# When a last convolution's two products run: the order of work in the inverse stage of a four-layer image kernel

## The chip, the core and the metric

One Trainium2 chip, one of its cores. The metric is the device time of one execution in microseconds (us); lower is better. The time before is a median of three runs, and the profile is of one further execution.

## The reference, cut to what matters

```python
def conv(x, z, ..., bias, L):              # layers 0, 1 and 3
    hx = _implicit_filter(z, Xw1, ..., deltas)
    hy = _implicit_filter(z, Yw1, ..., deltas)
    k = einsum('ijk,imk->ijmk', hx, hy)    # a separable filter for each channel
    ...
    y = irfft2(rfft2(x) * rfft2(k) / fft_size)[..., :L, :L]
    return y + x * bias[:, None, None]

def mix(x, v, conv_w, tau):                # layer 2
    f1 = haar2d(x)
    acc = 0
    for i in range(2):
        f4 = einsum('bchw,oc->bohw', f1 * v[i], conv_w[i])
        acc = acc + sign(f4) * relu(abs(f4) - tau[i])
    return haar2d(acc, inverse=True) + x

x = conv(x); x = conv(x); x = mix(x); x = conv(x)
```

x is (4, 64, 256, 256) in float32: 4 batches of 64 channels, each an image of 256 x 256. A convolution with a separable causal filter is two triangular Toeplitz products, one along each axis, with the channel's own filters.

## The kernel before, in words

**Tiling and stages.** A channel's image is a tile of 128 partitions x 2 x 256. A last convolution (layer 3, `last`, line 598) of one channel has five steps. The first product (`first`, line 256, due under the name "a3") contracts the image `u` with one of the channel's two Toeplitz filters into a PSUM bank `pa`; ScalarE copies it to SBUF as `a` ("a3 copy", line 267). The second product (`second`, line 271, "y3") contracts `a` with the other filter into a bank `py`; VectorE adds the image times its bias ("y3 sum", line 284), and ScalarE's queue starts the output's transfer ("out", line 602). Each product is `contract` (line 250): two halves, each with a matmul of 256 columns (line 253) and one of 128 (line 254). In the trace each of these is two passes, so a product is eight matmul records.

The work goes by batch. `convolutions` does layers 0 and 1 of a batch and the forward Haar transform, and leaves coefficients in DRAM (`coef`) and the images in `keep`. `mixing` mixes channels. `inverse` transforms back and does the last convolution. While batch b is mixed, layers 0 and 1 of batch b+1 run between its steps; the last eight channels of that are stretched over the first 36 ticks or so of the inverse stage of b. These late channels bring the steps "split" (ScalarE rounds to `sp`, line 361), "rest" (VectorE, line 366), "down" (a matmul into `pz`, line 373) and "away" (ScalarE copies `pz` to `co`, line 385, and SyncE's queue stores it), all due at n.73 of every third tick.

**The inverse stage** (`inverse`, line 509) has a tick for each of the 64 channels c, beginning at `start`. Steps of one channel, with the tick that they are due at: "sooner" c - 0.8 (SyncE's queue loads the filter tile `t`, line 244); "early" c - 0.4 (it loads `r`, line 515); "fetch" c + 0.414 (ScalarE gathers the channel's coefficients from `z` to `zc`, line 525); "rows" c + 1.071 (TensorE, lines 532 and 533, into `pw`); "join" c + 1.433 (VectorE, lines 554 to 558, makes the image `u`); then the last convolution. The first 16 channels have two steps more ("halves", "cols", lines 536 to 549), and their join and all after it are a tick later. Between these, VectorE does levels of the Haar transform on `z` (lines 291 and 292) for later channels.

In batches 0, 1 and 2 the channels 2, 5, 8, ... (`put_off`) do no last convolution here: `aside` puts `u` in DRAM (line 562), and `convolution` (line 605) does these 63 during the mixing of batch 3. So in three ticks there are two last convolutions. In batch 3 nothing is put off and each tick has one.

**What sets the order.** The author gives each step a due time in ticks, from the table `PLACE` and, for the last convolution, a shift by the channel's place in its group of three. All steps are sorted by due time and issued in that order (line 659). The framework turns this into one order per engine; there an instruction that isn't ready may be passed by a later one that is, so the due times act as priorities. After that each engine runs its own order and waits at each instruction. DMA triggers stand in the order of the engine that issues them: outputs and `late` in ScalarE's, loads and stores of `keep` and `coef` in SyncE's.

**Buffers that matter.** Four PSUM banks (tag "mm") serve all products, `pz` and "cols"; two pairs of banks serve rows and mixing. The copies `a` have two buffers ("mid"), images `u` five ("y"), filter tiles six ("toep"), and `r` three. The output tile of "y3 sum" and the coefficient tile of "away" share two buffers (tag "co").

Of the kernel before, what the change touches and what calls it, by code (L numbers as in the profile page):

```python
# [98 lines left out]
def conv_seq_kernel(ctx, tc, x, fz, fw, bias, decay, haar, haar_row, factors, vt, taut, wmix, out):  # L99
# [141 lines left out]
    def toeplitz(layer, c, name):  # L241

        t = tp.tile([P, 2, S], F32, name=name, tag="toep")
        nc.sync.dma_start(t, ap(pads[layer], c * 2 * ROW, [[1, P], [ROW, 2], [1, S]]))
        return t
# [48 lines left out]
    def level(n, chunk, begin=0, count=None):  # L294

        count = n if count is None else count
        v = z.rearrange("p n s x c -> p n s (x c)")[:, chunk].rearrange("p (j e s) x -> p j e s x", e=2, s=P // 2 // n)
        halve(v[:, begin : begin + count, 0, 0, :], v[:, begin : begin + count, 1, 0, :])

    def butterfly():  # L300

        v = z.rearrange("p n s (h k) c -> p n s h k c", k=2)
        for h in range(2):
            halve(v[:, :, 0, h, 0, :], v[:, :, 0, h, 1, :])
# [6 lines left out]
    def at(time, run, unit):  # L311
        events.append((time, len(events), run, unit))
# [196 lines left out]
    def inverse(b, start, put_off):  # L509

        st = {}

        def early(c):
            r = mx.tile([P, 2, 2, P], F32, name=f"r_{b}_{c}", tag="f", bufs=3)
            nc.sync.dma_start(r, keep[b][c])
            st[c]["r"] = r

        def sooner(c):
            st[c] = {}
            if c not in put_off:  # L520
                st[c][2] = toeplitz(2, c, f"t2_{b}_{c}")

        def fetch(c):
            a = mx.tile([P, 2, 2, P], F32, name=f"zc_{b}_{c}", tag="mag")
            nc.scalar.copy(a.rearrange("p h k i -> p (h k) i"), z[:, c // 16, :, :, c % 16].rearrange("p i x -> p x i"))  # L525
            st[c]["z"] = a

        def rows(c):
            a = st[c]["z"]
            ps = psx.tile([P, 2, 2, 2, P], F32, name=f"pw_{b}_{c}", tag="mix")[:, 0]  # L530
            for m in range(2):
                nc.tensor.matmul(ps[:, 0, m, :], a[:, 0, m, :], hsinv, start=True, stop=True)  # L532
                nc.tensor.transpose(ps[:, 1, m, :], a[:, 1, m, :], ident)  # L533
            st[c]["pw"] = ps

        def halves(c):
            w = st[c]["w"] = mx.tile([P, 2, 2, 2, P], F32R, name=f"w_{b}_{c}", tag="f4")
            ps = st[c]["pw"]
            nc.scalar.copy(w[:, 0], ps)
            nc.vector.tensor_tensor(w[:, 1], ps, w[:, 0].bitcast(F32), ALU.subtract)  # L540

        def cols(c):
            ps = psm.tile([P, 2, 2, P], F32, name=f"pu_{b}_{c}", tag="mm")
            flat = "p e m w -> p (e m w)"
            for i in range(2):
                nc.tensor.matmul(
                    ps.rearrange(flat), hb, st[c]["w"][:, i].rearrange(flat), start=(i == 0), stop=(i == 1)
                )
            st[c]["pw"] = ps

        def join(c):
            ps = st[c]["pw"]
            t = io.tile([P, 2, 2, P], F32, name=f"t_{b}_{c}", tag="res", bufs=BUFS["res"])
            nc.vector.scalar_tensor_tensor(t, st[c]["r"], 0.5, ps, ALU.mult, ALU.add)  # L554
            u = io.tile([P, 2, S], F32, name=f"u_{b}_{c}", tag="y", bufs=BUFS["y"])
            v = u.rearrange("p m (w e) -> p m w e", e=2)
            nc.vector.tensor_add(v[:, :, :, 0], t[:, 0], t[:, 1])  # L557
            nc.vector.tensor_sub(v[:, :, :, 1], t[:, 0], t[:, 1])  # L558
            st[c]["u"] = u

        def aside(c):
            nc.scalar.dma_start(late[b, c], st.pop(c)["u"])

        along = start - groups - 3

        def when(tick, n, chunk, *span):
            at(tick + PLACE["level"], lambda _: level(n, chunk, *span), 0)

        at(along + 11 + PLACE["level"], lambda _: butterfly(), 0)
        for chunk in range(1, 4):  # L570
            turn = start + 16 * (chunk - 1)
            for n in (1, 2, 4, 8):
                when(along + 12 + 3 * chunk if b + 1 < B else turn, n, chunk)
            when(turn + 1, 16, chunk)
            for i in range(2):
                when(turn + 2 + 2 * i, 32, chunk, 16 * i, 16)
            for i in range(4):
                when(turn + 6 + 2 * i, 64, chunk, 16 * i, 16)

        for c in range(C):  # L580
            for name, stage in zip(("sooner", "early", "fetch", "rows"), (sooner, early, fetch, rows)):
                at(start + c + PLACE[name], stage, c)
            turn = start + c
            if c < 16:
                at(start + c + PLACE["halves"], halves, c)
                at(start + c + PLACE["cols"], cols, c)
                turn += 1
            at(turn + PLACE["join"], join, c)
            if c in put_off:
                at(turn + PLACE["aside"], aside, c)  # L590
            else:
                shift = (0.0, -0.32) if c % 3 == 0 else (0.5, 0.18)
                if not put_off:
                    shift = (0.0, -0.5)
                for name, stage in zip(("a3", "a3 copy", "y3", "y3 sum", "out"), last(b, st)):
                    at(turn + PLACE[name] + shift[name[0] != "a"], stage, c)

    def last(b, st):
        return [
            *first(b, st, "u", 2, "a3"),  # L600
            *second(b, st, "a3", 2, "u", "y3", "co"),
            lambda c: nc.scalar.dma_start(out[b, c].rearrange("(k p) w -> p k w", p=P), st.pop(c)["y3"]),  # L602
        ]
# [19 lines left out]
    put_off = range(2, C, 3)  # L623
# [22 lines left out]
    for b in range(B):  # L646
        mixing(b, start, N_ACT[b])
        end = start + groups + 3
        if b + 1 < B:
            ready = convolutions(b + 1, spread(ahead, end + 2), in_parts=range(C), border=end)  # L650
        else:
            convolution(
                [(i, c) for i in range(B - 1) for c in sorted(put_off)], spread(start - 2, end + 2, (B - 1) * len(put_off))
            )
        inverse(b, end, put_off if b + 1 < B else ())

        start = max(end + C, ready + 3)
        ahead = start - 3
# [114 lines left out]
```

## Time and profile before

| | |
|---|---|
| median of 3 runs | 2916.31 us (2914.98 to 2917.72) |
| the profiled execution | 2915.48 us, its span 2913.7 us |
| granted TensorE clock | 1.0 |
| busy over the span: TensorE, VectorE, ScalarE, GpSimd | 2837.4, 2504.6, 2081.6, 329.1 us |
| inverse stage, first `zc` to last `zc`: batch 0 | 865.6 to 1056.6 us |
| batch 1 | 1517.7 to 1710.7 us |
| batch 2 | 2171.9 to 2365.9 us |
| batch 3 | 2662.4 to 2879.3 us |
| a copy `a` (line 267), fetch `zc` (line 525) | 0.587, 1.101 us (medians) |

How to read it: a row of the profile's groups has the line, the engine, the operation, what it writes and reads, and how often; then its busy time and the mean of one; then the idle time of that engine just before these instructions, and what ended most of it. PE is TensorE's matmuls, PEld its loading of weights, DVE is VectorE, ACT is ScalarE. Matmul records overlap by some 0.16 us[...].

### The profile page before, as it was taken

To read this page: it belongs to the slowest core of one execution; us is meant where nothing else is said; L and a number is where in the kernel's file an instruction comes from. 1 tells how busy PE (TensorE), PEld (TensorE's weight loads), DVE (VectorE), ACT (ScalarE), POOL (GpSimd) and SP (SyncE) were. 2 spreads that over 40 slices of the span, in tenths; PEclk is the share of its full clock that TensorE was granted. 3 is DMA by queue.
4 is the path that set the end of the run, shared out by engine and by line. 5 is a ranking of instruction groups with operands and counts; after the bars stand their busy time and mean duration, and the time that the engine had idled before them with its cause. 6 is when DMAs were issued, how large, how long until landed. Compare 5 with 4: busy or idle time off the path is not lost. (4 is left out here: it accounts for less than half of the span.)

```text
span 2913.7 us, 52472 instructions
## 1 busy us (share of the span) xinstructions
PE 2837.4 (97%) x16566; PEld 2548.3 (87%) x16566; DVE 2504.6 (86%) x4263; ACT 2081.6 (71%) x4950; POOL 329.1 (11%) x644
## 2 busy tenths in 40 slices
PE   8999999999999999999999999999999999999998
PEld 6899998888888898988898898988898898888887
DVE  4655558999999779999998779999998789999974
ACT  2333348999995558999986558999986568887443
POOL 0111111121120001212111001212111000000000
PEclk9999999999999999999999999999999999999999
DMA  5877777666677886776778886777778898876675
GB/s 163 259 231 229 231 236 218 205 207 205 200 209 231 277 251 199 212 214 209 211 215 252 265 249 200 213 213 207 212 215 255 260 266 230 238 228 204 206 227 168
DMA packets 599367, 649.77 MB, mean 223 GB/s; under 512 B 48465, under 2 KB 517044, under 8 KB 598964
## 3 DMA queue, kind: packets, MB, share of 16 engines
q1 hardware_dynamic: 519860, 562.09, 66.4%
q10 hardware_dynamic: 79232, 84.34, 8.2%
q8 instruction: 134, 2.20, 0.3%
q14 instruction: 141, 1.16, 0.1%
HBM read 426.77 MB, written 219.48 MB: 222 GB/s over the span
## 5 line engine op out<-in xcount | busy, mean ns | idle before, releaser
L253 PE MATMUL py<-t,a 128*128 128x256 f32 x3072 | 929.8, 384 | 32.1 <-ACT a L267 28.8
L267 ACT COPY a<-pa 128x512 f32<-128x512 f32 x768 | 491.4, 640 | 569.2 <-PE pa L254 511.3
L465 ACT ACTIVATE f<-px,vt 128x64 f32<-128x64 f32 x2816 | 622.2, 408 | 93.2 <-DVE f L460 93.0
L254 PEld LDWEIGHTS py<-t,a 128*128 128x128 f32 x3072 | 583.4, 190 | 79.4
L254 PE MATMUL py<-t,a 128*128 128x128 f32 x3072 | 590.1, 274 | 0.0
L253 PEld LDWEIGHTS py<-t,a 128*128 128x128 f32 x3072 | 494.9, 191 | 91.2 <-ACT a L267 59.7
L441 PE MATMUL px<-wb,f 128*128 128x256 f32 x2048 | 490.4, 381 | 11.4 <-ACT f L465 11.2
L441 PEld LDWEIGHTS px<-wb,f 128*128 128x128 f32 x2048 | 367.7, 190 | 56.7 <-ACT f L465 17.9
L343 POOL TENSOR_TENSOR sd<-less 128x128 f32<-128x128 f32 (+4 forms) x320 | 186.4, 583 | 1874.5 <-DVE less L342 1492.8
L469 ACT ACTIVATE mag<-f 128x1024 f32<-128x1024 f32 x256 | 304.3, 1189 | 20.8 <-DVE z L486 20.2
L476 DVE TENSOR_TENSOR mag<-mag,vt 128x1024 f32<-128x1024 f32 x256 | 311.7, 1218 | 5.0 <-ACT mag L469 4.0
L525 ACT COPY zc<-z 128x512 f32<-128x512 f32 x256 | 279.7, 1101 | 49.5 <-PE pw L533 38.0
L253 PE MATMUL pa<-t,y 128*128 128x256 f32 x1024 | 308.2, 383 | 5.6 <-DVE y L284 4.7
L480 DVE SCALAR_TENSOR_TENSOR mag<-mag,f 128x1024 f32<-128x1024 f32 x256 | 312.2, 1220 | 0.5 <-ACT f L472 0.4
L253 PE MATMUL pa<-t,x 128*128 128x256 f32 x1024 | 305.8, 380 | 0.0
L366 DVE TENSOR_TENSOR sp<-sd,sp 128x512 fp32r<-128x512 f32 x256 | 178.8, 698 | 146.7 <-ACT sp L361 144.2
L472 ACT ACTIVATE f<-f 128x1024 f32<-128x1024 f32 x256 | 291.5, 1139 | 3.2
L253 PE MATMUL pa<-t,u 128*128 128x256 f32 x772 | 231.4, 381 | 1.5 <-PE pw L533 0.7
L284 DVE SCALAR_TENSOR_TENSOR y<-x,bsb,py 128x512 f32<-128x512 f32 x256 | 189.5, 740 | 41.6 <-PE py L254 40.6
L284 DVE SCALAR_TENSOR_TENSOR y<-u,bsb,py 128x512 f32<-128x512 f32 x193 | 143.7, 745 | 91.2 <-PE py L254 70.1
L254 PEld LDWEIGHTS pa<-t,x 128*128 128x128 f32 x1024 | 194.6, 190 | 26.3
L254 PEld LDWEIGHTS pa<-t,y 128*128 128x128 f32 x1024 | 194.5, 190 | 26.3
(72 smaller groups left out, 4440.6 us busy)
## 6 DMA issues: line engine op xcount, KB each, us to landing
t<-pad SPq DMA_DIRECT2D x768, 256.0 KB, 4.1
x<-in_x SPq DMA_DIRECT2D x256, 256.0 KB, 3.8
coef<-co SPq DMA_DIRECT2D x256, 256.0 KB, 3.2
f<-coef SPq DMA_DIRECT2D x256, 256.0 KB, 3.2
r<-keep SPq DMA_DIRECT2D x256, 256.0 KB, 3.9
out_y<-y ACTq DMA_DIRECT2D x256, 256.0 KB, 4.1
keep<-sums SPq DMA_DIRECT2D x256, 128.0 KB, 2.8
keep<-sd SPq DMA_DIRECT2D x256, 128.0 KB, 2.9
```

The lines of the kernel that those rows point to most:

```text
L253: nc.tensor.matmul(ps[:, m, :], src[:, 0, m * P : (m + 1) * P], t[:, ::-1], start=True, stop=False)
L254: nc.tensor.matmul(ps[:, m, P:], src[:, 1, m * P : (m + 1) * P], t[:, : P - 1 : -1], start=False, stop=True)
L267: nc.scalar.copy(a, s["p" + new])
L284: nc.vector.scalar_tensor_tensor(y, s[res], bsb[:, layer, c : c + 1], s["p" + new], ALU.mult, ALU.add)
L343: engine.tensor_tensor(t[:, :, :, half:length], v[..., 0], v[..., 1], ALU.subtract)
L441: nc.tensor.matmul(ps[:, q, h, :], f[:, q, h * P : (h + 1) * P], wb.rearrange("p r n -> p (r n)"), start=True, stop=True,)
L465: nc.scalar.mul(f4[:, j], px[:, j], scale(g, 0)[:, j : j + 1])
L469: nc.scalar.activation(mag, st[g]["f4"], AF.Abs)
L472: nc.scalar.activation(st[g]["f4"], st[g]["f4"], AF.Sign)
L476: nc.vector.tensor_sub(mag, mag, over(g, 1, 16))
L480: nc.vector.scalar_tensor_tensor(mag, mag, 0.0, st[g]["f4"], ALU.max, ALU.mult)
L525: nc.scalar.copy(a.rearrange("p h k i -> p (h k) i"), z[:, c // 16, :, :, c % 16].rearrange("p i x -> p x i"))
```

## The change

Only the shifts of the last convolution's due times are changed.

```diff
-                shift = (0.0, -0.32) if c % 3 == 0 else (0.5, 0.18)
-                if not put_off:
-                    shift = (0.0, -0.5)
+                shift = (0.0, 0.0)
+                if put_off:
+                    shift = ((-0.27, -0.342), (0.23, 0.158))[c % 3]
                 for name, stage in zip(("a3", "a3 copy", "y3", "y3 sum", "out"), last(b, st)):
                     at(turn + PLACE[name] + shift[name[0] != "a"], stage, c)
```

The first number of a pair is for the first product and its copy, the second for the second product, its sum and the output. The due times that follow, for a channel c whose turn is c:

| | first product | its copy | second product and sum | output |
|---|---|---|---|---|
| batches 0 to 2, c % 3 = 0, before | c + 2.470 | c + 2.471 | c + 3.222 | c + 4.217 |
| after | c + 2.200 | c + 2.201 | c + 3.200 | c + 4.195 |
| batches 0 to 2, c % 3 = 1, before | c + 2.970 | c + 2.971 | c + 3.722 | c + 4.717 |
| after | c + 2.700 | c + 2.701 | c + 3.700 | c + 4.695 |
| batch 3, every c, before | c + 2.470 | c + 2.471 | c + 3.042 | c + 4.037 |
| after | c + 2.470 | c + 2.471 | c + 3.542 | c + 4.537 |

In batch 3 the second product of c is now due behind the first product of c + 1 (at c + 3.470), before it stood ahead of that. In batches 0 to 2, the copy of a first product with c % 3 = 0 is now due ahead of the fetch at c + 2.414, which it followed before, and the first product with c % 3 = 1 ahead of "split", "down" and "away" at c + 2.73, which it followed.

## The prediction, made before the changed kernel ran

> **What bounds the kernel now.** I read the page first, then the busy times by stage, then the waits of the last inverse stage, then the timeline of single ticks. The page names the engine:
>
> ```profile
> PE 2837.4 (97%) x16566; PEld 2548.3 (87%) x16566; DVE 2504.6 (86%) x4263; ACT 2081.6 (71%) x4950; POOL 329.1 (11%) x644
> ...
> L253 PE MATMUL py<-t,a 128*128 128x256 f32 x3072 | 929.8, 384 | 32.1 <-ACT a L267 28.8
> ...
> L253 PEld LDWEIGHTS py<-t,a 128*128 128x128 f32 x3072 | 494.9, 191 | 91.2 <-ACT a L267 59.7
> ```
>
> TensorE has next to no slack, and what idle time it has stands before `py`, the second product, waiting for ScalarE's copy `a` of the first. To see how much idle there is and where, I took the starts of all matmuls from the timeline and subtracted the spacing that unstalled ones show (0.216 us for 256 columns, 0.110 for 128). An unstalled product is 4 x 0.216 + 4 x 0.110 = 1.30 us, an unstalled `pw` (rows) 0.67. What is left over is TensorE's idle time: 123 us in the whole span, so no change of order can give more. The inverse stages, for which the change is made, hold: batches 0, 1, 2 from their 16th channel on (932 to 1062, 1582 to 1716, 2236 to 2371 us) 6.2, 9.6 and 10.7 us, of which the last third of each has 0.3, 0.3 and 0.9; their first 16 channels 6.2, 2.0 and 2.0; batch 3 (2662 to 2914) 3.8 for the first 16 channels and 22.2 for the rest. Batch 3 by stretches:
>
> ```profile
> 2713.00:2757.00 44.00, 40.96 (x253) 36.48 (x253) 42.25 (x69) 18.14 (x23) 0.00 (x0) 1.00 0.71 209
> 2757.00:2800.00 43.00, 42.09 (x269) 37.30 (x268) 41.23 (x68) 21.49 (x26) 0.00 (x0) 1.00 0.72 218
> 2800.00:2845.00 45.00, 44.24 (x283) 39.40 (x282) 27.97 (x52) 22.10 (x27) 0.00 (x0) 1.00 0.79 231
> 2845.00:2880.00 35.00, 34.35 (x215) 30.02 (x214) 21.67 (x40) 16.27 (x20) 0.00 (x0) 1.00 0.78 220
> 2880.00:2914.00 34.00, 25.24 (x146) 21.73 (x144) 11.84 (x20) 5.04 (x9) 0.00 (x0) 0.99 0.34 105
> ```
>
> The columns are the window, its length, then busy time of PE, PEld, DVE, ACT, POOL, the clock, DMA share, GB/s. To 2800 us VectorE is busy 83.5 of 87 us (the Haar levels on `z` run there): VectorE bounds. From 2800 it drops to 62% and TensorE bounds. My idle sums are 5.3, 3.6, 3.3, 3.3, 6.7. The waits of that part:
>
> ```profile
> DVE y L284 <- PE py L254: 47.1, 33, 2.9
> PEld py L253 <- ACT a L267: 18.2, 43, 0.9
> PE py L253 <- ACT a L267: 6.9, 12, 0.7
> ```
>
> and one tick with rows, then one after the last rows:
>
> ```profile
> 2881.75 0.38 PE L254 MATMUL pa<-t,u 128*128 128x128 f32 x2
> ...
> 2882.23 0.59 ACT L267 COPY a<-pa 128x512 f32<-128x512 f32 x1 [1.88 <-PE pa L254]
> ...
> 2882.87 0.70 PE L253 MATMUL py<-t,a 128*128 128x256 f32 x2
> ```
>
> ```profile
> 2893.71 0.30 PEld L253 LDWEIGHTS py<-t,a 128*128 128x128 f32 x2 [0.92 <-ACT a L267]
> 2893.71 0.70 PE L253 MATMUL py<-t,a 128*128 128x256 f32 x2 [0.73 <-ACT a L267]
> ```
>
> The reader is to see the order first product, rows, second product *of the same channel*. The copy starts 0.1 us after the product ends and takes 0.59; rows cover 0.67 of it, and 0.33 stay bare (0.23 of gap, and 0.10 for the first matmul after it). So the tick is 1.30 + 0.67 + 0.33 + 1.30 = 3.61 us, as the starts of `py` say (2839.49 to 2886.48 in 13 ticks). After the last rows nothing covers the copy, and the tick is 3.61 again with 1.0 us idle. In batches 0 to 2 there is a second pattern:
>
> ```profile
> 2288.98 0.75 DVE L284 SCALAR_TENSOR_TENSOR y<-u,bsb,py 128x512 f32<-128x512 f32 x1 [1.44 <-DMA coef<-co]
> ...
> 2289.76 0.38 ACTq L602 DMA_DIRECT2D out_y<-y  x1
> ...
> 2290.18 0.59 ACT L267 COPY a<-pa 128x512 f32<-128x512 f32 x1 [2.90 <-DVE y L284]
> ```
>
> The two `co` buffers are shared by outputs and by the coefficient stores of the next batch's last channels. A sum waits for a store to land, the output's trigger stands in ScalarE's order ahead of the copy, and TensorE waits 1.6 us behind both.
>
> **What the Trainium skill says.** PSUM — Partial Sum Buffer, section Engine vs sequencer instructions: ScalarE's and VectorE's queues are strictly first in first out, and matmuls start in program order. The trace agrees: the copy at 2290.18 follows the trigger at 2289.76 though its product ended before 2288.4. Perfetto Trace Analysis, section Identifying the Most-Contended Engine: matmul busy time is no measure of headroom, and it asks for the load of weights. Here PE is 97%, PEld 87%; I use neither but starts. Same page, section Matmuls: independent groups should rotate through PSUM banks so that one's evacuation overlaps the next one's matmuls. Before, only 0.67 us of rows lie over an evacuation.
>
> **The change part by part.** No instruction is added or removed. Due times are priorities: the trace has rows ahead of the second product, which is due first (n.042 against n.071) but is not ready.
>
> (1) Batch 3, second product, sum and output half a tick later. Second product of c is now due between first product of c+1 (n.47 against n.542) and rows (n.071 of the next). The copy it needs ended a tick earlier, so TensorE runs first(c+1), second(c), rows: 1.30 + 1.30 + 0.67 = 3.27 us for 3.61. From 2800 us on the idle is 3.3 + 3.3 + 6.7 = 13.3, the tail's six bare copies in it; I take 13 away. What hides the copy is now 1.3 us of product against 0.75 of copy with its latency; without it the 0.33 is back. The last channel's sum and output stay at the end, with the same length. From 2713 to 2800 idle is 8.9, but VectorE leaves 3.5 at most: I take 1 (bounds 0 and 3.5). First 16 channels: VectorE busy 48.8 of 51: 0.
>
> What is late next: VectorE has 2.27 us of work in a tick of 3.27 after the levels; ScalarE 0.59 + 1.10 + 0.38. Buffers: a copy tile of two is free because second(c-1) ended before first(c+1) does; a filter tile of six is held one tick longer, and its load (3.7 us to landing here) still has some four ticks. The output moves with the sum on ScalarE's queue: behind it stand the next copy and fetch; its sum ends 2.6 + 0.9 = 3.5 us into the tick, before the next first product ends (3.27 + 1.30), so nothing waits. Output landing is 3.6 us (2.2 in the tail); a buffer is wanted again after 2 x 3.27 - 0.78 = 5.8 (4.4 in the tail). SP's queue keeps its order, its waits for filter tiles fall with the second product. GpSimd has nothing here. DMA goes from 0.79 to some 0.87, below the 0.94 that other stretches reach.
>
> (2) Batches 0 to 2, first product and copy 0.27 earlier, second 0.022. On TensorE first, rows, second keep their order among themselves. For c%3 = 1 the first product (n.97 to n.70) passes the coefficient matmul `pz` (n.734), and its copy passes that channel's copy `co` and the split `sp` on ScalarE. For c%3 = 0 the copy passes the fetch, and the product the join's place, which is on VectorE and not in its way. For: the copy no longer waits for `co` 0.59 and `sp` 0.62 (stalls of about 0.9 at 2275.5), and `pz` (0.55) lies over it. Against: the coefficient store starts up to 1.30 + 0.59 = 1.9 us later, and it is the store that a sum waits for in the second pattern. There are 7 such matmuls in each window, 21 in all. Bounds: all idle outside the last thirds, 25 us, gained; or 21 x 1.9 = 40 lost. The trace can't say which buffer a sum will then take, the store's or the output's, which lands earlier. Going through one cycle with 4.7 us for a store and 4.2 for an output, I get a remaining stall of 0.8 where 1.2 stood: 0.43 each with the copy's share, 21 x 0.43 = 9. I take 9 gained.
>
> Sum: 13 + 1 + 9 = 23. The profiled execution took 2915.48 us (span 2913.7 and 1.8 around it): 2892.5. The median of the runs is 0.8 above it: **2893**.
>
> **The rivals.** *Batch 3 alone.* Part (2) does nothing: 13 + 1, so 2902. For it: TensorE's order is nearly the same in these stages, DMA is busy 0.83 to 0.94. Against: the copy plainly stands behind `co` and `sp`. *No effect.* Since due times are only priorities and ready work goes first, the emitted order could be the old one: 2916. Against: in batch 3 the second product is always ready when TensorE comes free, so it must go ahead of rows. *Slower.* The later coefficient store holds sums in the two `co` buffers, and ScalarE's queue stands behind their triggers. It decides when it costs more than 14 / 21 = 0.67 us each; at 1.15, some 60% of its bound, it costs 24 against 14: 2926.
>
> **How the numbers follow.** My sum has 0.62 (its own range 2880 to 2898), batch 3 alone 0.18, no effect 0.09, slower 0.11. 0.2% is 5.8 us, about what a measurement of this kernel can tell from no change; the first two lie beyond that: faster 0.80, same 0.10, slower 0.10 (a little of the last case falls within). The range leaves out the slower case and some of no effect above, and what lies below 2880, where more than 36 of the 47 us in reach (13.3 + 8.9 + 25) would have gone: 2880 to 2912.
>
> **What would show it.** Right: in the last stage the order is first, second, rows; ticks after the levels 3.27 us and the tail's 2.61; the waits of `py` for `a` in that part fall from 18.2 and 6.9 us to under 2 each; from 932 us on in batch 0 `co` comes after `a`. Wrong: a tail tick still 3.6; a new wait of `y` for out_y in batch 3; waits of `y` for coef above the present 5.8 us; or VectorE at 96% for longer than to 2800.

## The result, and the profile after

The changed kernel takes 2898.5 us (median of six runs, 2893.7 to 2901.0) beside 2915.6 for the kernel before on the same chip: a ratio of 0.9938, 95% interval 0.9925 to 0.995. That is 17 us less (18 by the ratio); the prediction said 23 less. The profiled execution took 2897.57 us, its span is 2895.8.

The page's lines for TensorE, after:

```profile
PE 2825.5 (98%) x16566; PEld 2548.3 (88%) x16566; DVE 2501.4 (86%) x4263; ACT 2082.3 (72%) x4950; POOL 335.3 (12%) x644
...
L253 PE MATMUL py<-t,a 128*128 128x256 f32 x3072 | 924.1, 383 | 18.6 <-ACT a L267 18.0
...
L253 PEld LDWEIGHTS py<-t,a 128*128 128x128 f32 x3072 | 495.9, 191 | 62.9 <-ACT a L267 31.7
```

The idle time before second products fell, from 32.1 to 18.6 us for the matmuls and from 91.2 to 62.9 for the loads of weights, but 18.0 and 31.7 us of waiting for a copy are left. The totals hide that two things happened. For each kernel I take an inverse stage from the last mixing matmul to the first of the next mixing (the last one to the end of the span). Lengths in us:

| | batch 0 | batch 1 | batch 2 | batch 3 |
|---|---|---|---|---|
| before | 215.5 | 219.2 | 216.4 | 264.6 |
| after | 217.3 | 223.7 | 215.6 | 242.2 |

Batch 3 gained 22.4 us, batches 0 to 2 together lost 5.5 in these two executions. Everything else moved by about 1 us. The last stage by windows, after, with the same columns as in the prediction (its start lies 4 us later than before):

```profile
2718.00:2762.00 44.00, 42.96 (x277) 39.05 (x276) 42.95 (x72) 21.57 (x27) 0.00 (x0) 1.00 0.73 223
2762.00:2805.00 43.00, 43.00 (x289) 40.09 (x288) 41.67 (x67) 21.98 (x27) 0.00 (x0) 1.00 0.80 238
2805.00:2850.00 45.00, 45.00 (x304) 42.17 (x303) 28.91 (x55) 22.88 (x28) 0.00 (x0) 1.00 0.80 241
2850.00:2880.00 30.00, 30.00 (x203) 28.12 (x202) 19.46 (x38) 15.57 (x19) 0.00 (x0) 1.00 0.78 240
```

TensorE is busy all through from 2762 to 2880 us, and in the first 43 of these VectorE is at 97%. Taken from the starts of its matmuls, TensorE's idle time from 2718 us to the end is 2.6 us, where 22.2 stood. The waits from 2718 us on:

```profile
ACT zc L525 <- PE pw L533: 58.9, 44, 1.4
DVE y L284 <- PE py L254: 33.0, 30, 1.9
ACT a L267 <- PE pa L254: 21.7, 47, 2.7
...
PEld pa L253 <- PE pw L533: 1.4, 2, 1.1
```

No wait of `py` for `a` is left in the list. What waits now is ScalarE and VectorE, for TensorE. One tick:

```profile
2826.01 0.60 PE L253 MATMUL pa<-t,u 128*128 128x256 f32 x2
...
2827.32 0.60 PE L253 MATMUL py<-t,a 128*128 128x256 f32 x2
...
2827.58 0.59 ACT L267 COPY a<-pa 128x512 f32<-128x512 f32 x1 [0.20 <-PE pa L254]
...
2828.63 0.39 PE L532 MATMUL pw<-hrow,zc 128*128 128x128 f32 x2
```

The second product starts at 2827.32, *ahead* of the copy at 2827.58, so it can't be that copy's: it belongs to the channel before. The tick is 3.28 us (first products at 2826.01 and 2829.30), and the tail's is 2.62 (2885.14 and 2887.76).

In batches 0 to 2 the sums wait longer for their buffers. The waits over the whole span, before and then after:

```profile
DVE y L284 <- DMA out_y<-y: 10.4, 12, 1.8
DVE y L284 <- DMA coef<-co: 5.8, 6, 1.5
```

```profile
DVE y L284 <- DMA out_y<-y: 23.3, 14, 5.4
DVE y L284 <- DMA coef<-co: 4.4, 3, 1.6
```

The longest of them, in batch 1:

```profile
1648.57 0.38 ACTq L602 DMA_DIRECT2D out_y<-y  x1
...
1653.37 0.27 PE L533 MATMUL pw<-hrow,zc 128*128 128x128 f32 x1
1656.59 0.75 DVE L284 SCALAR_TENSOR_TENSOR y<-u,bsb,py 128x512 f32<-128x512 f32 x1 [5.37 <-DMA out_y<-y]
...
1657.37 0.38 ACTq L602 DMA_DIRECT2D out_y<-y  x1
1657.79 0.59 ACT L267 COPY a<-pa 128x512 f32<-128x512 f32 x1 [4.95 <-DVE y L284]
```

An output started at 1648.57 lands only 8 us later. The next sum waits 5.4 us for its buffer, its trigger for the sum, the copy behind the trigger for 5.0, and TensorE stands still from 1653.6 to 1658.4. The path is the second pattern of the prediction, but the size looks like an accident of this execution: with the same due times in batches 0 to 2 alone (below), the longest such wait is 3.3 us. By the trace's semaphore events 15 of the output's 16 parts were done by 1652.77 and the last at 1656.49. Seven transfers in a row, loads and stores among them, had such a late last part, 2.5 to 3.9 us behind the others, and no other profile of this case has a row like it. So batch 1's 4.5 us can't all be charged to the new due times; what these cost has to come from the experiments.

### The profile page after: what moved, and what is told of

Its sections match the earlier page's. It is cut to its first block, busy times and chain, and to the rows that moved or that the text cites. A ratio compares the mean times of both kernels' runs of the same rounds, so it can differ in the third digit from the quotient of the medians.

```text
span 2895.8 us, 52461 instructions
## 1 busy us (share of the span) xinstructions
PE 2825.5 (98%) x16566; PEld 2548.3 (88%) x16566; DVE 2501.4 (86%) x4263; ACT 2082.3 (72%) x4950; POOL 335.3 (12%) x644
## 5 line engine op out<-in xcount | busy, mean ns | idle before, releaser
L253 PE MATMUL py<-t,a 128*128 128x256 f32 x3072 | 924.1, 383 | 18.6 <-ACT a L267 18.0
L253 PEld LDWEIGHTS py<-t,a 128*128 128x128 f32 x3072 | 495.9, 191 | 62.9 <-ACT a L267 31.7
L476 DVE TENSOR_TENSOR mag<-mag,vt 128x1024 f32<-128x1024 f32 x256 | 317.0, 1238 | 10.2 <-ACT mag L469 9.4
L284 DVE SCALAR_TENSOR_TENSOR y<-y,bsb,py 128x512 f32<-128x512 f32 x256 | 190.4, 744 | 27.8 <-PE py L254 27.8
```

What stands on the lines that cost most here:

```text
L253: nc.tensor.matmul(ps[:, m, :], src[:, 0, m * P : (m + 1) * P], t[:, ::-1], start=True, stop=False)
L284: nc.vector.scalar_tensor_tensor(y, s[res], bsb[:, layer, c : c + 1], s["p" + new], ALU.mult, ALU.add)
L476: nc.vector.tensor_sub(mag, mag, over(g, 1, 16))
```

## The experiments

All times are compared with the kernel before as it ran beside each, since its median was between 2915.6 and 2918.9 from one comparison to the next.

**Each part alone.** Batch 3 alone keeps the old shifts for the other batches:

```diff
-                    shift = ((-0.27, -0.342), (0.23, 0.158))[c % 3]
+                    shift = ((0.0, -0.32), (0.5, 0.18))[c % 3]
```

> Batch 3 has the new due times, batches 0 to 2 the old ones. Theory (the changed profile's stages add up: batch 3's inverse stage is 22 us shorter, the other three together 5.5 us longer): 22 us under the kernel before, some 2893. Rival (the longer stages of batches 0 to 2 are scatter of transfers and not the new due times): the same as the changed kernel, some 2898.

The other way round, with `shift = (0.0, -0.5)` for batch 3:

> Batches 0 to 2 have the new due times, batch 3 the old ones. Theory: these due times alone cost 5.5 us, so 2921. Rival (they do nothing): 2916. The prediction on record would have it at 2907.

Measured: batch 3 alone 2896.97 us, ratio 0.9919 (0.9906 to 0.9933), so 24 us less by the ratio and 22 by the medians. Batches 0 to 2 alone 2922.24 us, ratio 1.0012 (1.0003 to 1.002), 3 us more. The stage lengths in the order of the batches agree: 215.5, 220.1, 214.9, 242.3 for the first, 217.5, 222.3, 218.6, 264.3 for the second. What follows: the parts add up within 2 us, all of the gain is batch 3's, and the other part is a small loss where I had put a gain of 9.

**Is it the late part of batch 3 alone?** The prediction gave the stretch with Haar levels 1 us, since VectorE is 96% busy there, and the first 16 channels nothing. Here batches 0 to 2 have the old times, and in batch 3 only channels 0 to 31 have the new ones:

```diff
-                shift = (0.0, 0.0)
+                shift = (0.0, 0.0 if c < 32 else -0.5)
```

> Batches 0 to 2 old; in batch 3 only channels 0 to 31 have the new due times, which is the part in which VectorE is busy 96% of the time. Theory (VectorE doesn't bound there: its levels for later channels aren't due yet and slide, so TensorE's idle time counts there too): 8 to 10 us under the kernel before. Rival (the prediction on record: VectorE bounds until the levels are done): 1 us under it.

Measured: 2907.77 us beside 2917.82, ratio 0.997 (0.9958 to 0.9981): 10 us less (9 by the ratio), with batch 3's stage at 253.7. The half that I had written off holds nearly half of the gain. So 96% busy wasn't a bound that nothing could pass. The second test puts more work on VectorE, in batch 3 from channel 16 on, in the kernel with batch 3 alone:

```diff
-            nc.vector.tensor_sub(v[:, :, :, 1], t[:, 0], t[:, 1])
+            for _ in range(1 if put_off or c < 16 else 2):
+                nc.vector.tensor_sub(v[:, :, :, 1], t[:, 0], t[:, 1])
```

> Batch 3 alone with one more VectorE operation of 0.42 us (the last of the join done a second time, the values unchanged) for each channel of batch 3 from the 16th on. Theory (levels slide): 0 to 2 us over batch 3 alone. Rival (VectorE bounds until the levels are done, about channel 36): 20 x 0.42 = 8 us over it.

Measured: 2909.85 us, ratio 0.9971 (0.996 to 0.9983), some 14 us *over* batch 3 alone (by medians against their own runs of before: 8.0 less in place of 22.0). Both theories missed. Batch 3 alone, then the kernel with more VectorE work:

```profile
2718.00:2762.00 44.00, 42.82 (x276) 38.96 (x275) 42.97 (x74) 21.10 (x26) 0.00 (x0) 1.00 0.76 221
2762.00:2805.00 43.00, 43.00 (x291) 40.32 (x290) 41.20 (x66) 21.95 (x26) 0.00 (x0) 1.00 0.81 239
```

```profile
2718.00:2762.00 44.00, 38.46 (x225) 34.41 (x224) 40.29 (x69) 17.23 (x22) 0.00 (x0) 0.92 0.59 178
2762.00:2805.00 43.00, 36.54 (x234) 32.81 (x233) 41.14 (x69) 17.82 (x22) 0.00 (x0) 1.00 0.73 195
```

VectorE's busy time (the third pair) stays at 92 and 96% of the window, TensorE's falls by 4.4 and 6.5 us: here more work on VectorE does hold TensorE. From the 16th to the 32nd sum of batch 3, measured between the ends of sums, the three kernels do this (VectorE's time in levels, and the joins that ended):

| | us | VectorE idle | in levels | images joined |
|---|---|---|---|---|
| before | 57.0 | 1.4 | 24.4 | 17 |
| after | 50.7 | 1.2 | 21.1 | 15 |
| more VectorE work | 62.4 | 4.6 | 23.6 | 15 |

This is how both can hold. VectorE is full before and after, but with different work. Before, TensorE's waits made each channel slower, and VectorE filled that time with work ahead of need: 3.3 us more of levels, which are done by the 30th sum, and two joins more (1.5 us each) into free image buffers. After, it leaves that for later (the levels are done by the 35th sum, and from the 32nd to the 48th its idle time falls from 21.3 to 14.9 us), and 16 channels take 6.3 us less. So the change put work ahead of need off to later.

The added operation didn't do the same: there the levels are done by the 29th sum, and 16 x 0.42 = 6.7 us of it cost 11.6 us beside batch 3 alone (50.8). The rest shows as 2.2 us more of levels and 3.5 more of idle time. One stretch of slow clock, told of at the end, lies in these 16 channels, worth 1.7 us at most; another lies before them. Why the levels went ahead there isn't shown, and this profile is of the slowest of that kernel's six executions (2913.28 us). After the 32nd sum the same added operation costs nothing: 52.6 and 48.6 us for the next 16 and 15 channels, the same as without it.

**The two shared buffers.** A third buffer for outputs and coefficient stores, in the changed kernel (a constant's 0.5 KB a partition moves to make room, which the cut leaves out):

```diff
-BUFS = {"res": 1, "y": 5, "co": 2}
+BUFS = {"res": 1, "y": 5, "co": 3}
```

> The changed kernel with three buffers for outputs and coefficient stores in place of two (a constant of 0.5 KB is moved to make room). Theory (in batches 0 to 2 a sum waits for a buffer's transfer to land, the output's trigger on ScalarE's queue waits for the sum, and the copy of the next first product stands behind the trigger): waits of sums for out_y and coef fall from 23 us to under 3, the stages of batches 0 to 2 lose 10 to 15 us, 2885. Rival (TensorE waits there for rows and for the copy's own time, and buffers don't matter): 2898.

> Batch 3 new, batches 0 to 2 with the old due times, three buffers for outputs and stores. Theory (the new due times of batches 0 to 2 cost only by way of the two buffers): the same as the changed kernel with three buffers, 40 us under the kernel before, or up to 3 us slower, since the copy no longer stands behind the coefficient copy there. Rival (these due times cost whatever the buffers): 3 us or more under that kernel, 43 us under the kernel before.

> All due times of the kernel before, three buffers. Theory (the two gains are apart: the order in batch 3 22 us, the third buffer 18 to 20): 18 to 20 us under the kernel before. Rival (the third buffer helps only with the changed order): under 8 us.

Measured: the changed kernel with three buffers 2878.32 us, ratio 0.9855 (0.9842 to 0.9869); batch 3 alone with three 2872.20, 0.9839 (0.9825 to 0.9853), which is the fastest here; the old due times with three 2893.34, 0.9914 (0.9901 to 0.9927). In the changed kernel with three buffers no wait of a sum for `out_y` or `coef` is left in the list, where 23.3 and 4.4 us stood, and of second products waiting for copies this is left in the whole span, beside 31.7 and 18.0 us with two buffers (lines are one lower in this kernel):

```profile
PEld py L252 <- ACT a L266: 19.8, 43, 1.6
...
PE py L252 <- ACT a L266: 7.7, 13, 1.4
```

So the second pattern, which the prediction saw in the trace of before, is a matter of the buffers: a third one is worth 25 us with the old due times, more than either expectation gave it, and it adds to batch 3's order (25.5 alone and 22.0 alone, 46.7 together, by the medians). With the old due times 22 of the 25 lie in the stages of batches 0 to 2 (651.1 to 629.1 us). But it doesn't explain the loss of part two. With three buffers the stages of batches 0 to 2 sum to 628.6 us with the old due times and 634.1 with the new ones: 5.5 us, about as much as with two (650.5 and 656.6). These are single profiles: with two buffers the old due times gave 650.5 to 654.9 us in five of them, with three they gave 628.6 and 629.1. By time, the two intervals just overlap.

**Through which door does the late buffer hold TensorE?** Here the inverse stage's outputs of batches 0 to 2 are started from SyncE's queue, so no copy stands behind a trigger; two buffers, batch 3 alone:

```diff
-                for name, stage in zip(("a3", "a3 copy", "y3", "y3 sum", "out"), last(b, st)):
+                for name, stage in zip(("a3", "a3 copy", "y3", "y3 sum", "out"), last(b, st, nc.sync if put_off else nc.scalar)):
...
-    def last(b, st):
+    def last(b, st, queue=nc.scalar):
...
-            lambda c: nc.scalar.dma_start(out[b, c].rearrange("(k p) w -> p k w", p=P), st.pop(c)["y3"]),
+            lambda c: queue.dma_start(out[b, c].rearrange("(k p) w -> p k w", p=P), st.pop(c)["y3"]),
```

> Batch 3 alone, two buffers, and in batches 0 to 2 the outputs of the inverse stage are started by SyncE's queue instead of ScalarE's, so that no copy stands behind a trigger that waits for a late sum. Theory (TensorE is held through that place in ScalarE's order): 5 to 9 us under batch 3 alone. Rival (the load of filter tiles, now behind the trigger on SyncE's queue, comes late instead): over batch 3 alone by 2 us or more.

Measured: 2897.26 us, ratio 0.993 (0.9916 to 0.9944): nothing gained. The waits that moved, with batch 3 alone first:

```profile
PEld py L253 <- ACT a L267: 37.9, 64, 2.2
...
ACT a L267 <- DVE y L284: 16.5, 9, 3.0
...
DVE y L284 <- DMA out_y<-y: 10.2, 11, 1.8
```

```profile
PEld py L253 <- ACT a L267: 47.9, 129, 1.6
...
DVE y L284 <- DMA out_y<-y: 24.2, 20, 2.3
...
ACT a L267 <- DVE y L284: 1.0, 1, 1.0
```

The copy's wait for a sum did go (16.5 to 1.0 us), but sums wait 24.2 us for outputs in place of 10.2. So the trigger's place alone isn't what costs: with two buffers, taking it away only moved the wait. The rival isn't borne out either, at 0.3 us over. The edit also sets these triggers among SyncE's loads and stores, so it isn't the bare removal of one wait.

**Which channels cost?** Only channels with c % 3 = 1 get the new times, with two buffers and with three:

```diff
-                    shift = ((-0.27, -0.342), (0.23, 0.158))[c % 3]
+                    shift = ((0.0, -0.32), (0.23, 0.158))[c % 3]
```

> Batch 3 new; in batches 0 to 2 only channels with c % 3 = 1 have the new due times (their first product ahead of the coefficient matmul), those with c % 3 = 0 the old ones. Theory (the later coefficient matmul, copy and store are what costs): as the changed kernel, some 2898. Rival (the other channels' copy ahead of the fetch costs): as batch 3 alone, some 2893.

> Three buffers, batch 3 new; in batches 0 to 2 only channels with c % 3 = 1 have the new due times. With the old ones for all of them this kernel is 47 us under the kernel before, with the new ones for all 41. Theory (the cost of these due times comes from the channels with c % 3 = 0, whose first product and copy go ahead of the fetch: two thirds of it falls in the first 16 channels, where the copy delays the fetch and the split copy of a busy ScalarE and VectorE): 46 to 47 us under. Rival (it comes from the later coefficient matmul, c % 3 = 1): 41 to 43 us under.

Measured: with two buffers 2899.35 us, ratio 0.9929 (0.9916 to 0.9942), between the two expectations by the ratio. With three 2874.38 us, ratio 0.9863 (0.9847 to 0.988), by the ratio 40 us under the kernel before, beside 47 and 42 for old and new times, which is about the rival's figure. But the intervals overlap, and with two buffers the same edit's stages (649.4) show no loss. The waits of sums for outputs rise with this edit alone, from 10.2 to 20.9 us: that part is the later coefficient matmul's.

The two parts of a stage tell more. From the first to the 17th fetch, batches 1 and 2 take 64.0 to 64.5 us in all nine profiles in which the channels with c % 3 = 0 have the old times there, and 65.5 to 66.0 in the three in which they have the new ones (the two of the lag, below, aside), with two buffers as with three. So the new times of c % 3 = 0 cost over 1 us a batch in the first 16 channels, and no buffer count mends it; by which wait isn't shown. From the 17th fetch to the last, with three buffers, the three stages sum to 362.4 us with old times, 366.0 with c % 3 = 1 new and 364.6 with all new: by these single profiles, the new times of c % 3 = 1 cost 2 to 4 there. With two buffers this part varies from 383 to 388 with old times alone, too much to tell.

**The same order in all batches.** If a product between first and second is so good, batches 0 to 2 might have it too:

```diff
-                    shift = ((-0.27, -0.342), (0.23, 0.158))[c % 3]
+                    shift = ((0.0, 0.46), (0.5, 1.0))[c % 3]
```

> Batch 3 new; batches 0 to 2 with the second product behind the next first product as well (shifts 0.0, 0.46 and 0.5, 1.0), two buffers for outputs and stores. Theory (in batches 0 to 2 the buffers' transfers hold TensorE, but only through the copy that stands behind the trigger; with a product between, that copy has 1.3 us more): under batch 3 alone by 5 to 10 us. Rival (the sums themselves come late, and so the trigger and the copies by as much in each cycle): the same as batch 3 alone within 3 us.

> The same with three buffers. Theory: little is left to gain over the changed kernel with three buffers (TensorE's idle time there is small in batches 0 to 2), 0 to 6 us under it. Rival (filter tiles and images held longer make new waits): over it.

Measured: 2955.55 us, ratio 1.0131 (1.0117 to 1.0145), and with three buffers 2915.89, 0.9992 (0.9985 to 0.9998). By the medians against their own runs of before, that is 60 and 45 us worse than batch 3 alone with as many buffers, and both expectations missed. Some 47 and 30 us of it lie in the stages of batches 0 to 2, the rest mostly outside the inverse stages, where no run shows why. A new wait took the place of the old, with two buffers:

```profile
PEld pw L532 <- ACT zc L525: 38.4, 45, 1.7
...
PE pw L532 <- DVE t L554: 26.8, 14, 2.7
...
PE pw L532 <- ACT zc L525: 20.9, 34, 1.4
```

In these batches there are three rows to two convolutions. In the trace the four products now run together and the three rows after them in one go, each needing a fetch of 1.10 us and one of two `zc` buffers. Rows had been the filler between products, and fetches were hidden behind products. Both are lost; that this is the whole cost is argued from the order and the waits. In batch 3 each tick has one of each, and nothing bunches.

## Why the prediction was right, and where not

*Right in total, and in part by luck.* The forecast of 2893 is 5.5 us off, within its range, and the kernel is faster as said. But part one was 8 us too small and part two some 12 too large, and the two errors offset each other. The rival *Batch 3 alone*, 2902, lies nearer by the number (3.5 off), for no better reason: it has the same 14 for batch 3 and nothing for the rest.

*Part one, mechanism and tick: right.* First product, second of the channel before, rows; ticks of 3.28 (3.27 said) and 2.62 (2.61 said); no wait of `py` for `a` left; outputs, filter tiles and copies bring no new wait of weight. The 13 us after the levels are borne out: from the 32nd sum to the last, batch 3 takes 102.6 us in place of 116.1.

*The failed step of part one* is "VectorE leaves 3.5 at most: I take 1", for the stretch with levels. From the 16th to the 32nd sum it measured 6.3. I took a busy share for a bound, without asking whether that work was due. The trace of before had the answer: the last levels are done by the 30th sum, while the channels that need them are fetched from the 48th on. The same reasoning put the first 16 channels at 0; there it measured 2.6 (their sums end at 85.7 us from the stage's start in place of 88.3).

*The failed step of part two* is "a remaining stall of 0.8 where 1.2 stood", and so its sum, "21 x 0.43 = 9". It measured 3 lost. The order came as predicted: `co` and `sp` behind the copy, `pz` behind the first product. The next sum then takes the output's buffer, as the waits for `out_y` and `coef` show, but it waits longer: a sum that waits for either does so 0.9 us on average before, 1.6 after and 1.6 with batches 0 to 2 alone. What this longer wait itself costs TensorE isn't separated: the loss stays with three buffers, where no such wait is left. The other error is that the first 16 channels were put at nothing: from first to 17th fetch they lengthened by 0.2, 1.2 and 1.1 us in the three batches. The slower rival had the later store and the sign, but at a price of 24 us where 3 to 5 were lost, too little to decide.

## What to carry to other kernels

Where one engine is to be kept full, put an independent group of its own work between a producer and its consumer, but count what the old order used as filler: here it gained 22 us where each tick has one of each, and lost 45 and 60 us where there are three rows to two convolutions. A busy share of 96% needn't be a bound; look for when the results of that work are first needed. And before moving work around a wait, ask what ends it: a third buffer of 2 KB a partition gave more than the change.

## What the runs showed of the hardware

**A stall of TensorE costs more than its length.** The record of the granted clock shows stretches of 3.41 us at half speed around the end of long gaps between matmuls, a loss of up to 3.41 / 2 = 1.7 us each. After the gap in batch 1 of the changed kernel:

```profile
1640.00:1650.00 10.00, 9.96 (x65) 8.85 (x64) 6.79 (x14) 6.29 (x10) 0.00 (x0) 1.00 0.89 271
1650.00:1660.00 10.00, 5.22 (x31) 4.62 (x30) 4.43 (x10) 3.70 (x5) 0.00 (x0) 0.90 0.61 196
1660.00:1670.00 10.00, 10.00 (x65) 9.31 (x64) 6.76 (x13) 4.48 (x5) 0.00 (x0) 0.93 0.73 222
```

The column after POOL is the clock: 0.90 and 0.93, where it is 1.00 before. The gap was 5.05 us from start to start. The kernel with more VectorE work has three such stretches, after gaps of 3.08, 2.59 and 2.42 us, and the lag in all batches has eight. The Trainium skill, TensorE: Matmul & The Clock Gate, section HAM oscillation — how this bites in real kernels, gives the rule of no idle gaps over about 3.4 us. The length of the slow stretch agrees with that figure, but here shorter gaps were enough, and the measurement decides. Over all fourteen profiles, from 100 us on and from start to start, no gap under 2.3 us was followed by a slow stretch, of those from 2.3 to 2.7 some were and some weren't, and all five from 2.75 us on were. A gap of 2.32 or 2.33 us at some 760 us from the start is in each of the profiles of before, after and batch 3 alone, and of these three only the last has a slow stretch after it.

**Landing isn't one number.** An output of 256 KB landed in 2.2 us (median) in the tail of the kernel before, where 95 GB/s moved, in 3.6 from 2845 to 2880 us at 220 GB/s, and in 4.5 from 2330 to 2370 us at 284 GB/s. The 8 us of the stall in batch 1 are another matter: 15 of the transfer's 16 parts were done 4.2 us after its start, and the sum began at 1656.59, just after the last part, which came 3.7 us behind the others. With two buffers sums waited 16.2 us for landings in the kernel before; with three and the same due times the list has no such wait.
